# A state-space scan with the GpSimd product for four states at once, and the second step's inputs loaded first

## The chip, the cores and the metric

The kernel runs on one core of one Trainium2 chip. The metric is the device time of one execution in microseconds (us), of which the median over several runs is taken; lower is better. The engines are named as in the profile: PE is TensorE (matrix products), DVE is VectorE, ACT is ScalarE, POOL is GpSimd, SP is SyncE, which here issues every DMA.

## What is computed

Two layers of a network on images of 96 channels and 128 x 128 points, batch 2. The first layer mixes the points with a selective state-space scan (Mamba) along four orders of the points: rows, rows reversed, columns, columns reversed. Each order has 192 inner channels with 16 states each. Cut to the part that the change touches:

```python
def _mamba(x, in_w, conv_w, conv_b, xproj_w, dt_w, dt_b, A_log, Dp, outp_w):
    xz = x @ in_w.T
    xc, z = jnp.split(xz, 2, axis=-1)
    ...
    xc = jax.nn.silu((conv + conv_b[None, :, None]).transpose(0, 2, 1))
    xdbl = xc @ xproj_w.T
    ...
    dt = jax.nn.softplus(dt_raw @ dt_w.T + dt_b)
    A = -jnp.exp(A_log)
    def step(h, t):
        dt_t, u_t, B_t, C_t = t
        dA = jnp.exp(dt_t[:, :, None] * A)
        h = dA * h + dt_t[:, :, None] * B_t[:, None, :] * u_t[:, :, None]
        y = jnp.einsum('bds,bs->bd', h, C_t)
        return (h, y)
    ...
    y = ys.transpose(1, 0, 2) + Dp * xc
    y = y * jax.nn.silu(z)
    return y @ outp_w.T
```

A layer norm stands in front of it; the four results are projected, added and put on the input. A small two-layer network (FFN) with 8-bit products follows, then the second layer: a 3 x 3 convolution and a second FFN, each with a layer norm.

## The kernel before

For each of the two batches three stages run one after the other: `normalize` (layer norm, written to DRAM by rows as xnr and by columns as xnc), `mamba`, and `ffn_and_conv`. Nearly all of the time is in `mamba`.

**Steps and units.** `mamba` works in steps of 512 points (T). There are 64 steps in a batch: 32 blocks for the first pair of orders (rows and columns, forwards), then 32 for the second pair (backwards). The 2 x 192 channels of a pair of orders fill three groups (g = 0, 1, 2) of 128 partitions. A unit is two states of one group, so that a step has 24 units: group 0 is units 0 to 7, group 1 units 8 to 15, group 2 units 16 to 23. A quad is two units in a row, four states, starting at an even unit.

**What a unit does.** `decay` (L353): ScalarE makes two exponentials, dA, into a PSUM tile `da` of which there are three. `b_part`: GpSimd multiplies dt * u with a row of B in place (L345, 128 x 1024), and where the step is not the first of its pair it adds, with a small instruction (L347, 128 x 2), the decayed state of the step before to the first column. `scan` (L357): VectorE runs the recurrence along the 512 points, one instruction per state. `behind`: VectorE multiplies the states with the row of C (L431), ScalarE keeps the last column as the state for the next step (L432, `hst`), and TensorE sums the states of a group into y by products with the identity (L361, `sums`). For two units of each step, unit 2 and unit 10 (BY_POOL), the product with C is made by GpSimd (`by_pool`, L364), and their sums come three units later. At a group's end VectorE multiplies y with the gate (`gated`, L368), and TensorE and ScalarE project and collect it (L376, L378, L384).

**Rows.** B and C of a step lie in DRAM as rows (`bcd`); one DMA brings a quad of rows to all 128 partitions (L341, 1 MB). B has four such buffers and is fetched three quads ahead, C has three and is fetched two ahead. All DMAs stand in SP's one queue in the order of the program: in an even unit first the fetch of B, at its end the fetch of C.

**The prologue of a step** is the list `at` in `prologue`: the loads of its inputs (`load`, L220 or, for the first block, L218), three convolutions by products on TensorE (`conv`, L204), copied out by ScalarE (`conv_out`, L231), two silus (L251, L252 with the loads of their tables), B, C and dt from xc (L258, L264, L269, L276), the softplus in pieces on ScalarE (L281 to L292) and four small products of 512 columns per group on GpSimd (`dt_q`, `dt_log`, `dt_sum`, `dt_u`, L295 to L305), and the entering state (L310, L313). An entry (m, where, f) is put into unit m of the step before, so that a step's prologue runs under the scans of the step before it. Group 1 passes through a tile with its partitions in another order, `mix_xc` or `mix_sz`, and two DMAs put them in place (L248). Only the first step's prologue runs ahead of all scans, and the second step's, whose loads would belong to unit -2, is put in at unit 0.

**Order.** The order of instructions on each engine is written out by hand: it is the order in which the loop at the end of `mamba` calls them, unit after unit: the fetch of B, `feed` (b_part of the unit two ahead), the prologue's entries for place 0, the first scan, `behind` of the unit before, `feed_decay` (decay of the unit two ahead), the second scan, the fetch of C, and the entries for place 1. An instruction that waits holds up everything behind it on its engine.

Of the kernel before, what the change touches and what calls it, by code (L numbers as in the profile page):

```python
# [10 lines left out]
F32 = mybir.dt.float32  # L11
# [4 lines left out]
ALU = mybir.AluOpType  # L16
# [7 lines left out]
T = 512  # L24
# [10 lines left out]
AHEAD = 2  # L35
# [6 lines left out]
def tile_metaformer(ctx: ExitStack, tc: tile.TileContext, a: dict, out: bass.AP):  # L42
    nc = tc.nc
# [135 lines left out]
    def mamba(acc, xnr, xnc):  # L179

        with ExitStack() as st:
            pool = lambda n, bufs, **kw: st.enter_context(tc.tile_pool(name=n, bufs=bufs, **kw))
            io, one, two, gen = pool("io", 1), pool("one", 1), pool("two", 2), pool("gen", 4)
            ps_w, ps_y, ps_m = (pool(n, k, space=PSUM) for n, k in (("ps_w", 3), ("ps_y", 1), ("ps_m", 1)))
            rows_d = pool("rows_d", 3, space=DRAM)

# [1 line left out]
            enter = one.tile([128, NG, S], F32, name="enter")  # L188
# [18 lines left out]
            def prologue(pi, i, d):  # L207
# [19 lines left out]
                def conv_out(g):  # L227
                    if g == 1:
                        d["xc"] = two.tile([128, NG, T], F32, name="xc")
                    t = mixed("xc") if g == 1 else d["xc"][:, g, :]  # L230
                    nc.scalar.activation(t, d["ps"], AF.Identity, bias=convb[:, pi, g : g + 1])  # L231
# [4 lines left out]
                def gate_out(g):  # L236
                    if g == 1:
                        d["sz"] = two.tile([128, NG, T], F32, name="sz")
                    nc.scalar.copy(mixed("sz") if g == 1 else d["sz"][:, g, :], d["ps"])

                def mixed(name):
                    d["mix", name] = one.tile([128, T], F32, name=f"mix_{name}")
                    return d["mix", name]

                def mix(name):
# [89 lines left out]
            def row_tile(d, g, s, k, ahead):  # L335

                t = gen.tile([128, 4, T], F32, name=f"row{k}", bufs=ahead + 1)

                src = d["bcd"][k, s // 4] if g == 1 else d["bcd"][k, s // 4, g // 2 : g // 2 + 1]
                n = src.shape[0]  # L340
                nc.sync.dma_start(t, src[None].broadcast_to((128 // n, n, 4, T)))  # L341
                return t

            def b_part(i, d, g, s, b):
                nc.gpsimd.tensor_tensor(b, d["dtu"][g][:, None, :].broadcast_to((128, 2, T)), b, ALU.mult)  # L345
                if i > 0:
                    nc.gpsimd.tensor_tensor(b[:, :, 0], b[:, :, 0], enter[:, g, s : s + 2], ALU.add)  # L347

            def decay(pi, d, g, s):

# [5 lines left out]
            def scan(j, da, b, h):  # L356
                nc.vector.tensor_tensor_scan(h[:, j, :], da[:, j, :], b[:, j, :], 0.0, ALU.mult, ALU.add)  # L357
# [29 lines left out]
            steps = [(pi, i) for pi in range(2) for i in range(NT)]  # L387
            units = [(g, s) for g in range(NG) for s in range(0, S, 2)]
            nu = len(units)
            total = nu * len(steps)  # L390
            state = [{} for _ in steps]
            todo = {}

            def later(k, where, f, *args):
                todo.setdefault((k, where), []).append(partial(f, *args))

            def issue(k, where):
                for f in todo.pop((k, where), ()):
                    f()

            for k, where, f in prologue(*steps[0], state[0]):
                if k < nu:
                    f()
                else:
                    later(k - nu, where, f)
            bs, cs, das, hs = {}, {}, {}, {}

            def fetch(k, n, ahead, m):
                if k < total:
                    t = row_tile(state[k // nu], *units[k % nu], n, ahead)  # L410
                    m[k], m[k + 1] = t[:, 0:2, :], t[:, 2:4, :]

            def feed(k):
                if k < total:
                    n = k // nu
                    b_part(steps[n][1], state[n], *units[k % nu], bs[k])

            def feed_decay(k):
                if k < total:
                    n = k // nu  # L420
                    das[k] = decay(steps[n][0], state[n], *units[k % nu])
# [3 lines left out]
            def behind(k):  # L425

                n, u = divmod(k, nu)
                (pi, i), d, (g, s) = steps[n], state[n], units[u]
                h, c = hs.pop(k), cs.pop(k)
                if (g, s) not in BY_POOL:  # L430
                    nc.vector.tensor_tensor(c, h, c, ALU.mult)  # L431
                nc.scalar.copy(hst[:, g, s : s + 2], h[:, :, T - 1])  # L432
                if s == 0:
                    if k > 0:
                        pn, pu = divmod(k - 1, nu)
                        gated(steps[pn][0], state[pn], units[pu][0], ys.pop(k - 1))
                    y = ps_y.tile([128, T], F32, name="y")
                    nc.tensor.matmul(y, dmat[:, pi, g, :], d["xc"][:, g, :], start=True, stop=False)  # L438
                else:
                    y = ys.pop(k - 1)  # L440
                ys[k] = y
                if (g, s) in BY_POOL:
                    later(k + 1, 1, by_pool, h, c)
                    later(k + 3, 1, sums, s, y, c)
                else:
                    sums(s, y, c)
                if k == total - 1:
                    gated(pi, d, g, y)
                if s == S - 2 and g > 0:
                    later(k + 3, 0, project, pi, i, d, g)  # L450
                    later(k + 3, 1, collect, pi, d, g)

            for m, (n, ahead) in ((bs, (0, B_AHEAD)), (cs, (1, C_AHEAD))):
                for k in range(ahead):
                    fetch(2 * k, n, ahead, m)
            for k in range(AHEAD):
                feed(k)
                feed_decay(k)
            for k in range(total + 6):
                n, u = divmod(k, nu)  # L460

                ahead = 1 if k == 0 else n + 2 if u == nu - 2 else len(steps)
                if ahead < len(steps):
                    for m, where, f in prologue(*steps[ahead], state[ahead]):
                        later(max(k, (ahead - 1) * nu + m), where, f)
                if k % 2 == 0:
                    fetch(k + 2 * B_AHEAD, 0, B_AHEAD, bs)
                feed(k + AHEAD)
                issue(k, 0)
                if k < total:  # L470
                    (g, s) = units[u]
                    da, b = das.pop(k), bs.pop(k)
                    hs[k] = b if (g, s) in BY_POOL else da
                    scan(0, da, b, hs[k])
                if 0 < k <= total:
                    behind(k - 1)
                feed_decay(k + AHEAD)
                if k < total:
                    scan(1, da, b, hs[k])
                if k % 2 == 0:  # L480
                    fetch(k + 2 * C_AHEAD, 1, C_AHEAD, cs)
                issue(k, 1)
# [102 lines left out]
    for b in range(NB):  # L585
        xnr = dpool.tile([C, L], F32, name="xnr")
        xnc = dpool.tile([C, L], F32, name="xnc")
        normalize(b, acc, xnr, xnc)
        mamba(acc, xnr, xnc)
        ffn_and_conv(b, acc)  # L590
# [71 lines left out]
```

## Time and profile before

| What | Value |
|---|---|
| Median of 3 runs | 12191.46 us (12177.44 to 12192.11) |
| Profiled execution | 12201.18 us, its span 12199.4 us |
| VectorE busy over the span | 10961.9 us |
| GpSimd busy over the span | 10388.1 us |
| TensorE busy over the span | 10593.4 us |
| ScalarE busy over the span | 8592.7 us |
| First scan of batch 0 | 145.5 us into the span |
| First step of batch 0, first scan to the next step's | 96.1 us |
| Most frequent length of a step | 83.2 us |
| Mean granted TensorE clock | 0.975 |

A group's row in the profile reads: line, engine, operation, output<-inputs, shape, number; then the busy time of the group and the mean of one in ns; then the idle time of the engine just ahead of them and what ended most of it. A row of the timeline reads: start, duration, engine, line, operation, tiles, shape, number, and in brackets the idle time ahead of it with its releaser. A wait for several things is put down to the one that came last by the profile's records.

### The profile page before, as it was taken

To read this page: it belongs to the slowest core of one execution; us is meant where nothing else is said; L and a number is where in the kernel's file an instruction comes from. 1 tells how busy PE (TensorE), PEld (TensorE's weight loads), DVE (VectorE), ACT (ScalarE), POOL (GpSimd) and SP (SyncE) were. 2 spreads that over 40 slices of the span, in tenths; PEclk is the share of its full clock that TensorE was granted. 3 is DMA by queue.
4 is the path that set the end of the run, shared out by engine and by line. 5 is a ranking of instruction groups with operands and counts; after the bars stand their busy time and mean duration, and the time that the engine had idled before them with its cause. 6 is when DMAs were issued, how large, how long until landed. Compare 5 with 4: busy or idle time off the path is not lost. (4 is left out here: it accounts for less than half of the span.)

```text
span 12199.4 us, 100157 instructions
## 1 busy us (share of the span) xinstructions
PE 10593.4 (87%) x24208; PEld 4009.0 (33%) x24208; DVE 10961.9 (90%) x10624; ACT 8592.7 (70%) x15110; POOL 10388.1 (85%) x8360
## 2 busy tenths in 40 slices
PE   7888888888888888888978888888888888888889
PEld 2333333333333333333323333333333333333333
DVE  5999999999999999995469999999999999999954
ACT  6777777777777777765567777777777777777655
POOL 4999999999999999991159999999999999999911
PEclk8999999999999999999989999999999999999999
DMA  6887888888878878871068888878877878878700
GB/s 237 310 321 306 312 319 312 314 318 313 315 307 311 319 304 316 314 307 43 26 231 311 310 315 312 320 312 312 320 303 311 315 312 313 310 305 317 305 32 13
DMA packets 539204, 3417.36 MB, mean 280 GB/s; under 512 B 67276, under 2 KB 68396, under 8 KB 140696
## 3 DMA queue, kind: packets, MB, share of 16 engines
q1 hardware_dynamic: 538616, 3410.94, 72.5%
q8 instruction: 195, 3.19, 0.1%
q14 instruction: 393, 3.22, 0.1%
HBM read 3289.04 MB, written 54.53 MB: 274 GB/s over the span
## 5 line engine op out<-in xcount | busy, mean ns | idle before, releaser
L345 POOL TENSOR_TENSOR row<-dtu,row 128x1024 f32<-128x1024 f32 x3072 | 7235.6, 2356 | 262.2 <-DMA row<-bcd 212.3
L357 DVE TENSOR_TENSOR_SCAN da<-da,row 128x512 f32<-128x512 f32 x5632 | 6649.6, 1215 | 509.8 <-POOL row L347 166.1
L361 PE MATMUL y<-row,ident 128*128 128x512 f32 x12288 | 5956.1, 618 | 1135.8 <-DVE row L431 1131.4
L353 ACT ACTIVATE da<-dt,amat 128x512 f32<-128x512 f32 x6144 | 4249.9, 692 | 286.4 <-DVE row L357 99.3
L361 PEld LDWEIGHTS y<-row,ident 128*128 128x128 f32 x12288 | 2265.7, 193 | 4646.6 <-issue 2284.6
L431 DVE TENSOR_TENSOR row<-da,row 128x1024 f32<-128x1024 f32 x2816 | 3395.9, 1206 | 3.2 <-DMA row<-bcd 3.1
L432 ACT COPY hst<-da 128x2 f32<-128x2 f32 x2816 | 435.4, 155 | 1450.9 <-DVE row L431 1436.5
L204 PE MATMUL misc<-xa,inx 96*64 96x512 f32 (+1 forms) x2048 | 950.5, 607 | 133.1 <-DMA xa<-xnr 97.5
L556 POOL TENSOR_TENSOR acc<-acc,y 96x512 f32<-96x512 f32 x128 | 147.6, 1153 | 987.0 <-DVE y L555 972.6
L204 PE MATMUL misc<-xb,inx 96*64 96x512 f32 (+1 forms) x2048 | 949.7, 607 | 1.6 <-ACT xc L231 1.6
L347 POOL TENSOR_TENSOR row<-row,enter 128x2 f32<-128x2 f32 x2976 | 577.4, 194 | 233.4
L357 DVE TENSOR_TENSOR_SCAN row<-da,row 128x512 f32<-128x512 f32 x512 | 617.0, 1205 | 0.0
L364 POOL TENSOR_TENSOR row<-row,row 128x1024 f32<-128x1024 f32 x256 | 602.7, 2354 | 1.2 <-issue 0.6
L568 PE MATMUL pc<-pad,kw 96*96 96x512 f32 x1152 | 566.8, 593 | 0.0
L438 PE MATMUL y<-xc,dmat 128*128 128x512 f32 x768 | 432.1, 645 | 145.8 <-DVE sz L368 145.8
L295 POOL TENSOR_TENSOR q<-e,q 128x512 f32<-128x512 f32 x384 | 487.3, 1269 | 76.6 <-ACT q L292 71.5
L231 ACT ACTIVATE xc<-misc,convb 128x512 f32<-128x512 f32 x256 | 175.9, 687 | 525.8 <-PE misc L204 525.8
L204 PEld LDWEIGHTS misc<-xa,inx 96*64 96x64 f32 (+1 forms) x2048 | 326.8, 165 | 643.3 <-issue 470.1
L301 POOL TENSOR_TENSOR dt<-dt,ln 128x512 f32<-128x512 f32 x384 | 488.2, 1271 | 30.1
L298 POOL TENSOR_TENSOR ln<-ln,q 128x512 f32<-128x512 f32 x384 | 488.3, 1272 | 0.2
L305 POOL TENSOR_TENSOR dtu<-dt,xc 128x512 f32<-128x512 f32 x384 | 487.9, 1271 | 0.2
L378 PE MATMUL misc<-sz,gmat 128*96 128x512 f32 x1024 | 483.5, 594 | 0.0
(81 smaller groups left out, 9124.5 us busy)
## 6 DMA issues: line engine op xcount, KB each, us to landing
row<-bcd SPq DMA_DIRECT2D x3072, 1024.0 KB, 7.0
xc<-mix_xc SPq DMA_DIRECT2D x256, 128.0 KB, 5.3
sz<-mix_sz SPq DMA_DIRECT2D x256, 128.0 KB, 5.4
xa<-xnr SPq DMA_DIRECT2D x124, 193.1 KB, 5.3
xb<-xnc SPq DMA_DIRECT2D x124, 193.1 KB, 5.5
bcd<-rows SPq DMA_DIRECT2D x128, 128.0 KB, 6.5
acc<-in_x_dram SPq DMA_DIRECT2D x16, 768.0 KB, 8.6
xnr<-xn SPq DMA_DIRECT2D x16, 768.0 KB, 4.3
```

The lines of the kernel that those rows point to most:

```text
L204: nc.tensor.matmul(ps[rows, :], w(PAIRS[pi][d], k, lo, hi), src[d][:, k : k + T], **se)
L298: nc.gpsimd.tensor_tensor(d["ln"], d["ln"], d["q"], ALU.add)
L301: nc.gpsimd.tensor_tensor(d["dt"][g], d["dt"][g], d["ln"], ALU.add)
L305: nc.gpsimd.tensor_tensor(dtu, d["dt"][g], d["xc"][:, g, :], ALU.mult)
L345: nc.gpsimd.tensor_tensor(b, d["dtu"][g][:, None, :].broadcast_to((128, 2, T)), b, ALU.mult)
L347: nc.gpsimd.tensor_tensor(b[:, :, 0], b[:, :, 0], enter[:, g, s : s + 2], ALU.add)
L353: nc.scalar.activation(da[:, j, :], d["dt"][g], AF.Exp, scale=amat[:, pi, g, s + j : s + j + 1])
L357: nc.vector.tensor_tensor_scan(h[:, j, :], da[:, j, :], b[:, j, :], 0.0, ALU.mult, ALU.add)
L361: nc.tensor.matmul(y, ident, c[:, j, :], start=False, stop=s + j == S - 1)
L364: nc.gpsimd.tensor_tensor(c, h, c, ALU.mult)
L431: nc.vector.tensor_tensor(c, h, c, ALU.mult)
L568: nc.tensor.matmul(pc, kw[:, t, :], rows, start=t == 0, stop=t == 8)
```

## The change

GpSimd's `b_part` handles a quad: one product of 128 x 2048 and one add of 128 x 4, called only in even units, in front of that unit's prologue entries. The two mix tiles become one. The pool of the inputs xa and xb has two buffers, and the entries of a step's prologue that fall ahead of unit 0, which are the second step's loads, are issued at once, ahead of the first fetches of rows. Entries of later steps keep their units.

```diff
--- before.py
+++ after.py
@@ -180,7 +180,7 @@
 
         with ExitStack() as st:
             pool = lambda n, bufs, **kw: st.enter_context(tc.tile_pool(name=n, bufs=bufs, **kw))
-            io, one, two, gen = pool("io", 1), pool("one", 1), pool("two", 2), pool("gen", 4)
+            io, one, two, gen = pool("io", 2), pool("one", 1), pool("two", 2), pool("gen", 4)
             ps_w, ps_y, ps_m = (pool(n, k, space=PSUM) for n, k in (("ps_w", 3), ("ps_y", 1), ("ps_m", 1)))
             rows_d = pool("rows_d", 3, space=DRAM)
 
@@ -239,7 +239,7 @@
                     nc.scalar.copy(mixed("sz") if g == 1 else d["sz"][:, g, :], d["ps"])
 
                 def mixed(name):
-                    d["mix", name] = one.tile([128, T], F32, name=f"mix_{name}")
+                    d["mix", name] = one.tile([128, T], F32, name="mix")
                     return d["mix", name]
 
                 def mix(name):
@@ -342,9 +342,9 @@
                 return t
 
             def b_part(i, d, g, s, b):
-                nc.gpsimd.tensor_tensor(b, d["dtu"][g][:, None, :].broadcast_to((128, 2, T)), b, ALU.mult)
+                nc.gpsimd.tensor_tensor(b, d["dtu"][g][:, None, :].broadcast_to((128, 4, T)), b, ALU.mult)
                 if i > 0:
-                    nc.gpsimd.tensor_tensor(b[:, :, 0], b[:, :, 0], enter[:, g, s : s + 2], ALU.add)
+                    nc.gpsimd.tensor_tensor(b[:, :, 0], b[:, :, 0], enter[:, g, s : s + 4], ALU.add)
 
             def decay(pi, d, g, s):
 
@@ -403,17 +403,31 @@
                     f()
                 else:
                     later(k - nu, where, f)
-            bs, cs, das, hs = {}, {}, {}, {}
+
+            def prepare(n):
+                if n < len(steps):
+                    for m, where, f in prologue(*steps[n], state[n]):
+                        k = (n - 1) * nu + m
+                        if k < 0:
+                            f()
+                        else:
+                            later(k, where, f)
+
+            prepare(1)
+            bs, cs, das, hs, quads = {}, {}, {}, {}, {}
 
             def fetch(k, n, ahead, m):
                 if k < total:
                     t = row_tile(state[k // nu], *units[k % nu], n, ahead)
                     m[k], m[k + 1] = t[:, 0:2, :], t[:, 2:4, :]
+                    if n == 0:
+                        quads[k] = t
 
             def feed(k):
+
                 if k < total:
                     n = k // nu
-                    b_part(steps[n][1], state[n], *units[k % nu], bs[k])
+                    b_part(steps[n][1], state[n], *units[k % nu], quads.pop(k))
 
             def feed_decay(k):
                 if k < total:
@@ -453,19 +467,17 @@
             for m, (n, ahead) in ((bs, (0, B_AHEAD)), (cs, (1, C_AHEAD))):
                 for k in range(ahead):
                     fetch(2 * k, n, ahead, m)
+            feed(0)
             for k in range(AHEAD):
-                feed(k)
                 feed_decay(k)
             for k in range(total + 6):
                 n, u = divmod(k, nu)
-
-                ahead = 1 if k == 0 else n + 2 if u == nu - 2 else len(steps)
-                if ahead < len(steps):
-                    for m, where, f in prologue(*steps[ahead], state[ahead]):
-                        later(max(k, (ahead - 1) * nu + m), where, f)
+                if u == nu - 2:
+
+                    prepare(n + 2)
                 if k % 2 == 0:
                     fetch(k + 2 * B_AHEAD, 0, B_AHEAD, bs)
-                feed(k + AHEAD)
+                    feed(k + AHEAD)
                 issue(k, 0)
                 if k < total:
                     (g, s) = units[u]
```

## The prediction

> **What bounds the kernel now.** I read the busy shares first, then the costliest groups, then a table of stretches, then the timeline of one step engine by engine, because the shares alone name two engines at once.
>
> ```profile
> PE 10593.4 (87%) x24208; PEld 4009.0 (33%) x24208; DVE 10961.9 (90%) x10624; ACT 8592.7 (70%) x15110; POOL 10388.1 (85%) x8360
> ...
> L345 POOL TENSOR_TENSOR row<-dtu,row 128x1024 f32<-128x1024 f32 x3072 | 7235.6, 2356 | 262.2 <-DMA row<-bcd 212.3
> L357 DVE TENSOR_TENSOR_SCAN da<-da,row 128x512 f32<-128x512 f32 x5632 | 6649.6, 1215 | 509.8 <-POOL row L347 166.1
> ...
> L347 POOL TENSOR_TENSOR row<-row,enter 128x2 f32<-128x2 f32 x2976 | 577.4, 194 | 233.4
> ```
>
> ```profile
> 1000.00:2000.00 1000.00, 874.15 (x1985) 331.02 (x1986) 964.31 (x871) 727.89 (x1289) 955.23 (x776) 0.99 0.80 313
> ```
>
> In a scanning stretch (columns: PE, its loads, VectorE, ScalarE, GpSimd) VectorE is busy 96%, GpSimd 96%, TensorE 87%. The largest named wait of the scans is for GpSimd's small add (166.1 us). This looks like a kernel that a faster GpSimd would help by up to 510 us. The timeline of one step says otherwise. I take the step whose first scan is at 2003.94; the next one's is 83.2 later, and 66 of the 122 undisturbed steps take 83.2 within 0.1. Times "into the step" count from that scan. The step's three VectorE stalls:
>
> ```profile
> 2017.96 1.23 DVE L357 TENSOR_TENSOR_SCAN da<-da,row 128x512 f32<-128x512 f32 x1 [0.86 <-POOL row L347]
> ...
> 2025.56 1.23 DVE L357 TENSOR_TENSOR_SCAN da<-da,row 128x512 f32<-128x512 f32 x1 [0.76 <-POOL row L347]
> ...
> 2036.45 1.23 DVE L357 TENSOR_TENSOR_SCAN da<-da,row 128x512 f32<-128x512 f32 x1 [0.68 <-ACT hst L432]
> ```
>
> The first two (units 4 and 6) are GpSimd's. The third, unit 9, is there in every step at 0.4 to 0.7 us, also where the first is missing. What ends it is on TensorE and ScalarE:
>
> ```profile
> 2019.65 3.60 PE L204 MATMUL misc<-xa,inx 96*128 96x512 f32 x8
> 2023.09 1.88 PE L361 MATMUL y<-row,ident 128*128 128x512 f32 x4
> 2024.80 3.60 PE L204 MATMUL misc<-xb,inx 96*128 96x512 f32 x8
> ```
>
> ```profile
> 2028.44 0.69 ACT L231 ACTIVATE xc<-misc,convb 128x512 f32<-128x512 f32 x1 [1.43 <-PE misc L204]
> 2029.03 0.15 ACT L432 COPY hst<-da 128x2 f32<-128x2 f32 x1
> 2029.21 1.42 ACT L353 ACTIVATE da<-dt,amat 128x512 f32<-128x512 f32 x2
> 2030.65 1.28 ACT L251 ACT_TABLE_LOAD   x1
> ...
> 2034.93 1.42 ACT L353 ACTIVATE da<-dt,amat 128x512 f32<-128x512 f32 x2
> ```
>
> TensorE has no idle time from 2.4 to 41 us into the step: the last sums of the old step, three convolutions, a projection and the sums of units 0 to 6. Its third convolution ends at 24.4, ScalarE copies it out, makes one decay, does the silu (4.1 us with its two table loads) and only then the decay of unit 9, ready at 32.4; the scan starts at 32.5. So from product 23 of the old step (1.1) to scan 9 (32.5) runs a chain of 31.4 us in which GpSimd has no part. Unit 6 is held by it as well: its decay is ready at 21.5, the scan started at 21.6. From scan 9 to the next product 23 VectorE runs without a gap, 51.8 us. Chain and run are 83.2: the period.
>
> GpSimd meets this period with room to spare:
>
> ```profile
> 2039.26 2.35 POOL L345 TENSOR_TENSOR row<-dtu,row 128x1024 f32<-128x1024 f32 x1 [0.74 <-DMA row<-bcd]
> ```
>
> Before unit 12 it waits for rows (35.4 into the step, mean 1.7 over the steps). Their load stands in SP's queue behind a load that waits for TensorE's sums of units 2 and 3 (28.3), again the chain.
>
> **The Trainium skill.** Its page "GPSIMD Engine Reference", section 3.1 Elementwise, gives 4497 ns for a tensor_tensor add of 2048 fp32 elements. The trace has no such size, but 1271 ns at 512, 2356 at 1024 and 194 at 2: 2.12 ns an element and 187 fixed, so 4.52 us; they agree. Its page "Perfetto Trace Analysis", section GPSIMD Engine Instruction, advises start-to-start spacing for GpSimd, which I use: product and add come every 2.58 us. Its page "DMA: Bandwidth & Descriptors", section Anatomy of one DMA, says a semaphore wait is held by the issuing sequencer before dispatch; the trace agrees, with SP's 5297.7 us of waiting on TensorE in one queue.
>
> **The change part by part.** 1. *Quads.* Two products and two adds (2 x 2.58 = 5.16 us) become 4.52 + 0.08 gap + about 0.15 = 4.75; saved 0.41 to 0.45 a quad, 12 quads, about 5 us of GpSimd's 82 per step. The price is granularity: the even unit waits for 4.75 instead of 2.58. With GpSimd's order and spacings (small products 1.22 to 1.3, by_pool 2.3) the quad's readiness against its first scan in the 83.2 us step, starting from the rows at 35.5:
>
> unit 12: 40.3 against 42.2; 14 (behind by_pool): 47.3 / 49.0; 16: 52.2 / 55.7; 18 (behind three small products): 60.8 / 63.0; 20: 66.8 / 69.7; 22: 75.4 / 76.5; next step's 0: 81.6 / 83.2; 2: 87.5 / 90.5; 4: 96.1 / 96.1; 6: 103.2 / 102.9; 8: 108.1 / 109.9; 10: 112.9 / 118.6; then rows at 118.7 again.
>
> Only unit 6 is 0.3 late, where ScalarE's decay is later still (104.7). So the 2.4 us of GpSimd stall at units 4 to 6 go, and the same time comes back as waits for ScalarE at 5, 6 and 9. Gain in an 83.2 us step: nothing. If the chain cover were gone it would be up to 2.4 us a step.
>
> 2. *Steps where GpSimd is late elsewhere.* Going through the scans, 12 steps lose 0.5 to 1.4 us at units 21 to 23 to the small add, 11.8 us in all. There VectorE is exposed. Putting their own row times into the list above, the worst quad is 0.0 to 0.1 late at unit 22 and 0.3 at 14: some 10 to 12 us gained; bounds 0 and 14.
>
> 3. *Late inputs.* Some 35 steps are longer because TensorE waits for xa (0.1 to 3.9 us each). The second buffer does not help: in the instruction order of both kernels the load of every later step stands at the same place of SP's queue, and in before it waits there for no reader of the old buffer; it is issued 2 us ahead of the step and lands 5 to 10 us later. Gain 0; bounds -10 and +10.
>
> 4. *The second step's inputs.* In before they are issued behind seven row loads of 1 MB:
>
> ```profile
> 138.03 3.70 SPq L341 DMA_DIRECT2D row<-bcd  x7
> 141.83 0.42 SPq L220 DMA_DIRECT2D xa<-xnr  x1
> ```
>
> ```profile
> 159.14 1.09 PE L204 MATMUL misc<-xa,inx 96*64 96x512 f32 x1 [14.74 <-DMA xa<-xnr]
> ```
>
> ```profile
> 168.32 1.23 DVE L357 TENSOR_TENSOR_SCAN da<-da,row 128x512 f32<-128x512 f32 x1 [9.70 <-ACT da L353]
> ```
>
> TensorE stands 14.7 us, ScalarE behind it (10.8 in front of L231), VectorE behind that. The first step takes 96.1 us in batch 0, 95.3 in batch 1; without stalls VectorE needs 79.7 (first unit has no gate). Stalls there: 1.4, 9.7, 1.2, 2.3, 1.0, and 0.1 restarting after each. In after, the two loads (0.45 us each to issue, 0.39 MB, 1 us at the 2.48 us per MB of the landings) go ahead of the rows: rows 1 us later, first quad 2.2 later than the first pair: first scan 3.1 us later. The convolution can start when ScalarE frees the misc bank, about 147.5 instead of 159.1. Left over are ScalarE waits: in the first step it has two extra dt groups (4 us each) and two silus by unit 12, about 34 us in VectorE's 30 up to unit 9, of which two units of lead cover most: 2 to 3 us. Gain 16.4 - 3.1 - 2.5 = 10.8 us, twice: 21.6; bounds 14 and 26.
>
> 5. *One mix buffer for both.* The 512-column tile is written at units 2 and 13 and its two copies land within some 5 us: 35 us of slack, cost 0. Waits of the state copies on DMAs disappear; they cost nothing now.
>
> Sum: 0 + 11.8 + 0 + 21.6 = 33.4 us. Profiled execution 12201.18 - 33.4 = 12168; that execution is 9.7 above the median of the runs, so 12191.46 - 33 = 12158.
>
> **Rivals.** A: *GpSimd was the bound.* For it: the named waits of 166 us and 96% busy. Then the 2.4 us a step go, 126 x 2.4 = 300: about 11870. Against: unit 9's wait in every step, TensorE without a gap. Chance 0.08. B (slower): *the quad gates VectorE at units 12 to 22*, where nothing covers. The smallest lead is 1.1 at unit 22, six quads after the rows; it is used up when a quad costs 0.18 more, 4.9 with its add. At 5.1 it would be 1.0 to 1.2 us a step, +140 - 22: about 12310. For it: a size never traced, and DMA jitter: rows land up to 2 us late in a tenth of the steps, 7 in the worst. Against: a straight line through three sizes. Chance 0.12. C: *the start gives nothing net* because ScalarE's load and the later first quad eat it: 12180 or so. Chance 0.12.
>
> **Numbers.** The forecast has 0.68. A difference of 0.2% (24 us) is about what a measurement can tell from no change; the forecast is 33 +- 12, beyond it nine times in ten. Faster 0.61 + 0.08 = 0.69, same 0.07 + 0.11 = 0.18, slower 0.13. The forecast alone spans 12130 to 12185; with C and the lesser degrees of A and B, 12100 to 12198.
>
> **What would show it.** Right: L345 x1536 at about 4.5 us; steps still 83.2 apart; fewer waits of L357 for the add, more for ScalarE; unit 9's stall near 2 to 3 us; first steps near 85 us; xa waits fewer by two, of 14 us. Wrong: periods under 82 (A); waits for the add at units 12 to 22 (B); first steps over 92 (C).

## The result, and the profile after

| | before | after |
|---|---|---|
| Median | 12194.74 us (20 runs, 12177.44 to 12248.8) | 12164.91 us (20 runs, 12131.31 to 12198.56) |
| Ratio to before | | 0.9971, 95% interval 0.9961 to 0.9981 |

By the medians the change gains 29.8 us; 33 were forecast. The ratio in the table is not the quotient of the two medians (0.9976); by it the gain is 35 us, with an interval from 23 to 48. The two profiled executions hide this: their spans are 12199.4 and 12196.8 us, because the profiled execution of after, 12198.56 us, is the slowest of its 20. So the traces are compared stretch by stretch and step by step, not by their spans.

First the page of after: busy time by engine, then the groups that answer to those shown of before.

```profile
PE 10601.0 (87%) x24208; PEld 4012.8 (33%) x24208; DVE 10962.5 (90%) x10624; ACT 8585.5 (70%) x15110; POOL 9908.7 (81%) x5336
...
L345 POOL TENSOR_TENSOR row<-dtu,row 128x2048 f32<-128x2048 f32 x1536 | 6949.9, 4525 | 820.8 <-DMA row<-bcd 658.5
L357 DVE TENSOR_TENSOR_SCAN da<-da,row 128x512 f32<-128x512 f32 x5632 | 6650.2, 1215 | 509.8 <-ACT da L353 187.3
```

A quad costs 4525 ns, as the straight line through three sizes said. GpSimd has 479.4 us less work (10388.1 to 9908.7) and stands idle for most of it: its products now wait 658.5 us for rows instead of 212.3. The idle time of these scans is 509.8 us, as before. That it agrees to the tenth is chance: the first two steps of the batches lost 28 us of it and the last ones 2, while the waits ahead of the two first scans grew by 10 and the steps between by 20, through inputs that came late (below). What the change did in the usual step is to put other names behind the idle time, which the view of VectorE's waits shows best (who waited, for whom, us in total, times, the longest). After:

```profile
DVE da L357 <- ACT da L353: 187.3, 190, 3.6
DVE da L357 <- ACT hst L446: 157.8, 124, 1.6
DVE da L357 <- POOL row L345: 103.3, 6, 51.8
...
DVE da L357 <- POOL row L347: 49.8, 100, 1.0
```

The wait for the small add fell from 166.1 to 49.8 us, and the two waits for ScalarE rose from 88.9 and 72.8 to 187.3 and 157.8. The timeline of VectorE in one step of after, whose first scan is at 2000.60, has its stalls at the same three units as before (4, 6 and 9):

```profile
2014.01 1.23 DVE L357 TENSOR_TENSOR_SCAN da<-da,row 128x512 f32<-128x512 f32 x1 [0.25 <-POOL row L347]
...
2022.23 1.23 DVE L357 TENSOR_TENSOR_SCAN da<-da,row 128x512 f32<-128x512 f32 x1 [1.38 <-ACT hst L446]
...
2033.03 1.23 DVE L357 TENSOR_TENSOR_SCAN da<-da,row 128x512 f32<-128x512 f32 x1 [0.59 <-ACT da L353]
```

Into the step these are 13.4, 21.6 and 32.4 us; in before they were 14.0, 21.6 and 32.5. Unit 4 starts 0.6 us sooner and loses it at unit 6, which starts at the same moment in both kernels. The usual step is 83.13 us against 83.20. In all of the 122 steps between the batches' starts and ends, unit 6 now waits for ScalarE (1.28 us in the mean) and so does unit 9 (0.59 us); GpSimd's add is still what ends the stall at unit 4 in 91 of them. GpSimd's own order came out as worked out: in this step the quads of units 12, 16, 18 and 22 are ready at 40.2, 52.2, 60.9 and 75.5 us, where the prediction's list has 40.3, 52.2, 60.8 and 75.4.

Most of what was gained is at the start of each batch. VectorE's timeline of after, first scan, and then the two stalls of the first step that are left up to unit 9 (a third, of 0.45 us, comes at unit 22):

```profile
151.40 3.61 DVE L357 TENSOR_TENSOR_SCAN da<-da,row 128x512 f32<-128x512 f32 x3 [51.78 <-POOL row L345]
...
176.89 1.23 DVE L357 TENSOR_TENSOR_SCAN da<-da,row 128x512 f32<-128x512 f32 x1 [0.43 <-POOL row L345]
...
180.81 1.23 DVE L357 TENSOR_TENSOR_SCAN da<-da,row 128x512 f32<-128x512 f32 x1 [0.44 <-ACT da L353]
```

The 9.70 us stall is gone. By the distances of the steps' first scans, the first steps take 80.8 us in both batches (96.1 and 95.3 before) and the second ones 83.1 (84.5 and 84.4).

### The profile page after: what moved, and what is told of

Its sections match the earlier page's. It is cut to its first block, busy times and chain, and to the rows that moved or that the text cites. A ratio compares the mean times of both kernels' runs of the same rounds, so it can differ in the third digit from the quotient of the medians.

```text
span 12196.8 us, 95712 instructions
## 1 busy us (share of the span) xinstructions
PE 10601.0 (87%) x24208; PEld 4012.8 (33%) x24208; DVE 10962.5 (90%) x10624; ACT 8585.5 (70%) x15110; POOL 9908.7 (81%) x5336
## 5 line engine op out<-in xcount | busy, mean ns | idle before, releaser
L345 POOL TENSOR_TENSOR row<-dtu,row 128x2048 f32<-128x2048 f32 x1536 | 6949.9, 4525 | 820.8 <-DMA row<-bcd 658.5
L357 DVE TENSOR_TENSOR_SCAN da<-da,row 128x512 f32<-128x512 f32 x5632 | 6650.2, 1215 | 509.8 <-ACT da L353 187.3
L124 DVE TENSOR_TENSOR xq<-xm,rs 96x512 fp8e5<-96x512 f32 x128 | 87.9, 687 | 388.0 <-ACT rs L120 387.9
```

## The experiments

The two theories: TensorE's and ScalarE's chain sets the step, so that only the start gains; or GpSimd's work sets it, so that the quads gain. Ratios are to before, each measured beside it on the same chip. "Usual step" is the most frequent length, read from the first scans of the 122 steps that are neither at a batch's start nor at its end. The median of before moved between 12189.86 and 12201.45 us from one session to the next, so a difference between the medians of two experiments is good to some 10 us only.

**The early loads alone.** Second input buffer, one mix tile, early loads; b in pairs.

```diff
 # after.py
-                nc.gpsimd.tensor_tensor(b, d["dtu"][g][:, None, :].broadcast_to((128, 4, T)), b, ALU.mult)
+                nc.gpsimd.tensor_tensor(b, d["dtu"][g][:, None, :].broadcast_to((128, 2, T)), b, ALU.mult)
...
-                    nc.gpsimd.tensor_tensor(b[:, :, 0], b[:, :, 0], enter[:, g, s : s + 4], ALU.add)
+                    nc.gpsimd.tensor_tensor(b[:, :, 0], b[:, :, 0], enter[:, g, s : s + 2], ALU.add)
...
                     fetch(k + 2 * B_AHEAD, 0, B_AHEAD, bs)
-                    feed(k + AHEAD)
+                feed(k + AHEAD)
```

> The early loads, the second input buffer and the one mix tile, with b still made in pairs. Theory (TensorE and ScalarE set the step, the start is what is gained): the first scan 3 to 4 us later, the first step near 82 us instead of 96, twice; 20 to 28 us faster than before, ratio about 0.998; waits of the scans for the small add stay near 166 us. Rival (GpSimd's work sets the step, the quads are what is gained): 5 us or less, ratio 0.9995 to 1.

Measured: 12185.14 us, ratio 0.9991 (0.9984 to 0.9999); 16 us gained by the medians, beside 12201.45, and 11 by the ratio. First scan at 150.2, first steps 82.7 and 82.6 us, usual step 83.20, the wait for the small add 152.1 us. The direction and the place are those of the theory; the size is under the 20 to 28 us expected, in part because the first scan comes 4.7 us late instead of 3 to 4. It is more than the rival allows, but the interval reaches to it.

**The quads alone.** The loads and buffers of before, b in quads as in the change's diff.

```diff
 # before.py
-                nc.gpsimd.tensor_tensor(b, d["dtu"][g][:, None, :].broadcast_to((128, 2, T)), b, ALU.mult)
+                nc.gpsimd.tensor_tensor(b, d["dtu"][g][:, None, :].broadcast_to((128, 4, T)), b, ALU.mult)
...
-                feed(k + AHEAD)
+                    feed(k + AHEAD)
```

> The quads alone, with the loads and buffers of before. Theory: the usual step stays at 83.1 to 83.2 us, GpSimd's waits are exchanged for ScalarE's; 2 us lost at each start, 6 to 12 us gained in the steps where GpSimd was late at units 21 to 23: 0 to 12 us faster, ratio 0.999 to 1.000; first steps still about 95 us. Rival (GpSimd sets the step): 25 us or more faster, ratio 0.998 or less.

Measured: 12177.55 us, ratio 0.9981 (0.9971 to 0.9991), 24 us gained, where 0 to 12 were expected. That is a miss upwards, and by the total alone the rival, which named 25 us or more, is nearer. The steps tell what the trace can account for. The usual step is 83.13 us: 0.07 for 122 steps are 8.5 us, which no step of the prediction had. First scan at 147.7, 2.2 late as worked out; the first steps 93.4 and 93.2 us, 2 to 3 less than in before, the second ones 83.2 and 83.1. Together that is about 12 to 14 us, inside the interval (11 to 35 us) at its low end; where the rest comes from, if it is there, is open. The product of this ratio and the one above is 0.9972, so within the noise the two halves add up to the whole. Neither theory's claim to all of the gain stands; but the quads' share doesn't come out of the stalls at units 4 and 6. The wait for the small add fell to 57.0 us, and the waits for ScalarE took its place:

```profile
DVE da L357 <- ACT hst L434: 158.0, 124, 1.7
DVE da L357 <- ACT da L353: 156.1, 172, 9.1
DVE da L357 <- POOL row L345: 96.8, 4, 48.8
DVE da L357 <- POOL row L347: 57.0, 114, 1.3
```

**Less work for GpSimd, no quads.** The small add is left out of before, so the entering state is not in the scans.

```diff
 # before.py
-                if i > 0:
-                    nc.gpsimd.tensor_tensor(b[:, :, 0], b[:, :, 0], enter[:, g, s : s + 2], ALU.add)
```

> Before with GpSimd's small add (L347) left out, so that the state of the step before does not enter the scans; 0.23 us less of GpSimd per unit, 5.4 us per step, without the quads' coarser grain. Theory: the usual step stays at 83.2 us, only the late steps gain, 10 to 20 us in all, ratio 0.9984 to 0.9992. Rival (GpSimd sets the step): the 2.4 us of stall a step go, 250 to 300 us, ratio 0.976 to 0.98.

Measured: 12191.43 us, ratio 0.9988 (0.9980 to 0.9995), as expected. The usual step is 83.20 us, to the hundredth that of before, though GpSimd has the 577 us of the small adds less to do. Its groups and VectorE's waits:

```profile
L345 POOL TENSOR_TENSOR row<-dtu,row 128x1024 f32<-128x1024 f32 x3072 | 7187.3, 2356 | 1035.3 <-DMA row<-bcd 819.3 <-DVE sz L366 199.7 <-ACT hst L430 9.7
L355 DVE TENSOR_TENSOR_SCAN da<-da,row 128x512 f32<-128x512 f32 x5632 | 6642.6, 1214 | 508.4 <-POOL row L345 202.1 <-ACT da L351 150.8 <-ACT hst L430 84.0
```

GpSimd's work turned into waiting for rows (212.3 to 819.3 us), and the scans' idle time did not move (509.8 to 508.4). A wait put down to GpSimd's product is still the largest name; it is no cause, as the step did not get shorter. Unit 9 waits 0.67 us in all of the 122 steps (0.6 us in 121 of them in before). This is what rules out GpSimd as the bound of before.

**The inputs sooner.** After, with each later step's inputs loaded at unit -8 instead of -2; the second buffer allows it.

```diff
 # after.py
-                at = [(-2, 1, load), (2, 1, partial(mix, "xc")), (6, 1, partial(silu, "xc"))]
+                at = [(-8, 1, load), (2, 1, partial(mix, "xc")), (6, 1, partial(silu, "xc"))]
...
-                if u == nu - 2:
+                if u == nu - 8:
```

> After with each later step's inputs loaded at unit -8 instead of -2, which the second buffer allows. Theory (steps over 83.2 us come from xa landing late, up to 6.7 us a step): TensorE's waits for xa vanish but for the two at the batches' starts, at least 115 of 122 steps are under 83.5 us, 80 to 130 us faster than after, 110 to 160 faster than before, ratio 0.987 to 0.991. Rival (the lateness is of all DMAs and comes up elsewhere, in rows): under 40 us faster than after, ratio over 0.994, with waits of GpSimd or VectorE for rows in its place.

Measured: 12078.82 us (12073.04 to 12081.04), ratio 0.9897 (0.9881 to 0.9913): 86 us under after by the medians, 90 by the ratios. The view of TensorE's waits has two for the inputs left, at the two batches' starts. In after it had 33, two of them at the starts:

```profile
PE misc L204 <- DMA xa<-xnr: 108.0, 33, 28.4
```

With the inputs sooner:

```profile
PE misc L204 <- DMA xa<-xnr: 28.4, 1, 28.4
PE misc L204 <- DMA xb<-xnc: 28.3, 1, 28.3
```

107 of the 122 steps are within 0.3 us of the usual 83.13 (71 in after), a few under the 115 expected. The time lost ahead of unit 9, over that of the usual step, fell from 122 to 2 us; what is left over is 9 us behind it, nearly all at unit 22 and GpSimd's. The lateness did not come up elsewhere. The spread of the runs fell from 67 us (20 runs) to 8 (5 runs): late inputs are most of what makes executions of after differ. The mean granted clock goes along with this: it went from 0.973 to 0.978 over the runs of after, lower in the longer ones, and was 0.977 or 0.978 in all five here. The edit doesn't touch it, but which of the two drives the other isn't shown.

**A shorter chain, in pairs and in quads.** Inputs at unit -10; the first convolution is made at unit -2, where TensorE has idle time, the second at 1, the third at 4 instead of 5; the move of the first through the mix tile comes sooner with it. Once with pairs (early-only kernel), once with quads (after).

```diff
-                at = [(-2, 1, load), (2, 1, partial(mix, "xc")), (6, 1, partial(silu, "xc"))]
+                at = [(-10, 1, load), (-1, 1, partial(mix, "xc")), (6, 1, partial(silu, "xc"))]
...
-                for g, k in ((1, 1), (0, 3), (2, 5)):
+                for g, k in ((1, -2), (0, 1), (2, 4)):
...
-                if u == nu - 2:
+                if u == nu - 10:
```

> b in pairs, as in the early-only kernel, with the inputs loaded at unit -10 and the first and third convolutions taken out of TensorE's crowded stretch (first at unit -2 instead of 1, second at 1 instead of 3, third at 4 instead of 5). Theory: the chain that set the step is about 2.5 us shorter, so the step falls until GpSimd, 82.3 us of work with pairs, sets it: usual step 82.3 to 83.0 us, waits of the scans for the small add grow over 166 us; 12010 to 12080 us, ratio 0.984 to 0.990. Rival (the chain isn't what sets the step, or VectorE alone is): 83.2 or 80.5 us a step with pairs and quads alike.

> The same moves with the quads of after. Theory: GpSimd needs only 77 us, so the step falls to VectorE's 80.3 us and what is left of ScalarE's waits: usual step 80.4 to 81.6 us, 1 to 2.4 us a step under the pairs' kernel, 11760 to 11900 us, ratio 0.964 to 0.976; the quads, worth some 20 us before, are worth 120 to 290 here. Rival (quads are worth nothing with this order either): within 30 us of the pairs' kernel.

Measured: pairs 11962.37 us, ratio 0.9815 (0.9801 to 0.9828); quads 11860.28 us, ratio 0.9730 (0.9717 to 0.9744). The steps are 82.1 us in the mean with pairs and 81.3 with quads, the usual steps 82.15 and 81.0. The pairs' kernel is some 50 us faster than expected, and the quads' advantage is 102 us, under the 120 of the range: GpSimd's need with pairs, set at 82.3 us a step, is 82.1 or less. The kernel with the inputs sooner alone kept the usual step of 83.13 us and is 218 us slower than the quads' kernel here, so the shorter step is the convolutions' doing and not the inputs'. The stretch from 1000 to 2000 us (PE, its loads, VectorE, ScalarE, GpSimd), pairs first:

```profile
1000.00:2000.00 1000.00, 884.28 (x2019) 334.11 (x2018) 983.72 (x889) 745.39 (x1312) 974.20 (x793) 0.99 0.83 320
```

```profile
1000.00:2000.00 1000.00, 897.03 (x2034) 338.90 (x2033) 992.90 (x899) 754.17 (x1330) 937.31 (x503) 0.98 0.84 323
```

With pairs GpSimd is busy 97.4%, and what is left is not waiting: its products wait for rows 33.0 us in the whole run, 28 of them at the starts. VectorE's and GpSimd's waits with pairs:

```profile
DVE da L357 <- POOL row L347: 111.7, 242, 1.3
...
POOL row L345 <- DMA row<-bcd: 33.0, 10, 14.1
```

The scans wait for the add at units 4 and 6 alone. In total these waits are under before's 166 us, where over 166 were expected: here GpSimd does set the step, and the waits named after it are fewer than in before, where it didn't. With quads VectorE is busy 99.3% and the wait for the add is 32.5 us. With the chain out of the way, the same quads are worth 102 us. The quads' kernel is the fastest of all, 2.5% under after.

**A quad that costs more.** After, with a spare GpSimd product behind each quad's add.

```diff
 # after.py
+            spare = one.tile([128, 128], F32, name="spare")
+            nc.gpsimd.memset(spare, 0.0)
...
                     nc.gpsimd.tensor_tensor(b[:, :, 0], b[:, :, 0], enter[:, g, s : s + 4], ALU.add)
+                nc.gpsimd.tensor_tensor(spare, spare, spare, ALU.mult)
```

> After with one more GpSimd product of 128 x 128 on a spare tile behind each quad's add, about 0.46 us a quad (estimated from the rows at 2, 512 and 1024 columns), 5.5 us a step: GpSimd then has as much work as in before, in quads. Theory of the exposed places: at unit 22 five of these, 2.3 us, stand against a lead of 1.1, and nothing covers there: usual step 84.2 to 84.8 us with waits for the add at unit 22, 130 to 200 us slower than after, 12290 to 12370 us, ratio 1.008 to 1.014. Rival (a quad has slack to spare as GpSimd's total of 83 us is under the step): usual step 83.1 to 83.3 us, under 30 us slower than after, ratio 0.997 to 1.000.

Measured: 12314.36 us, ratio 1.0108 (1.0091 to 1.0125): 149 us over after's median. The spare product took 399 ns, where the line through other sizes had given 0.46 us. Groups and waits of that kernel:

```profile
L350 POOL TENSOR_TENSOR spare<-spare 128x128 f32<-128x128 f32 x1536 | 612.2, 399 | 0.0
```

```profile
DVE da L360 <- POOL row L349: 391.6, 320, 2.0
DVE da L360 <- POOL row L347: 111.4, 10, 51.4
```

In 120 of the 122 steps unit 22 waits for the add, 0.90 us each, 108 us in all. Most of the rest of the 391.6 us, 231 at unit 4 and 40 at unit 6, lies in the stretch from unit 4 to unit 9, where ScalarE holds the scans too. The 75 steps in which TensorE doesn't wait for inputs are 84.35 us in the median, as expected: some 1.0 us over after's behind unit 9 and 0.3 ahead of it. All 122 steps are 85.0 us in the mean. So 0.4 us a quad turn the change into a loss, most of it at unit 22, where the list of the prediction had its smallest lead without cover, although GpSimd's whole work is only 1.3% over that of before (9908.7 + 612.2 us against 10388.1).

## Why the prediction was right

- *The bound.* Right. The step is set by TensorE's convolutions, ScalarE's silu and the decays behind them. Shown from both sides: less work for GpSimd left the step at 83.20 us; a shorter chain brought it to 81.0. The experiments moved only the convolutions; ScalarE's part of the chain is read from the timelines.
- *Quads.* Cost right (4.52 foretold, 4525 ns), and so is the argument that nothing is gained at units 4 to 6. One detail was wrong: unit 9's stall was to grow to 2 or 3 us; it stayed 0.59. Unit 6, which the text had as held by ScalarE too, takes all of the time back.
- *0.07 us a step*, 8.5 us in all, was not foreseen. The kernels with quads and the old order have it, and none of those with pairs. At unit 9 the scan starts 0.03 us after its decay instead of 0.10. In before the scan of an odd unit also waits for GpSimd, in after for ScalarE alone; that this is the cause is argued, not shown.
- *Steps with GpSimd late.* Mis-sized: 10 to 12 us expected; the loss at units 9 to 23 went from 12.7 to 9.0 us. The lead at unit 22 was put at -0.1 to 0.0 in such steps, and it is -0.4 to -0.7 in nearly all of after's.
- *Late inputs.* Right that the second buffer doesn't help: TensorE waits for xa 33 times in after, 35 in before. The time lost ahead of unit 9 is 122 us in after's profiled execution and 90 in before's, a difference as large as the change. But after's execution lies 33.7 us over its median and before's 6.4; without that some 88 and 84 us would be left (an estimate), which are alike.
- *The start.* The sum is right by luck, as its terms are not: first scan 5.9 us later (3.1 expected), stalls left in the first step about 1 us (2.5 expected), and the second step 1.3 us shorter, which was not in the working. In batch 0: 5.9 - 15.3 - 1.3 = -10.7 us, against the -10.8 of the sum. The first rows take 7.1 us from issue to landing behind the two input loads, instead of about 5. The sign "first steps near 85 us" does not fit the prediction's own terms either, which make 79.7 + 2.5 = 82.2; it was 80.8.
- *Sum.* Start 22, usual step 8.5, late steps 3.7: 34 us, where the medians show 29.8 and the ratio 35. The working had 21.6, 0 and 11.8. That the total came out so near is in part luck, as the last two miss in opposite directions. The experiments split it otherwise than the working too: 16 us for the early loads alone, with 20 to 28 expected, and 24 for the quads alone, with 0 to 12 expected.

## What to carry to other kernels

A wait's name says what came last there, not what sets the pace: look for the stall that is in every period, also where the named one is missing, and follow that one back. Taking work from an engine that isn't on this chain turns into idle time on it; the same saving was worth 24 us with the chain in place and 102 us with it shortened and the inputs sooner. When a buffer is added, ask what it now allows to be moved: issuing the inputs six units sooner was worth 86 us more, over twice the whole change.

## What was not expected of the hardware

The input loads of a step, 0.39 MB, were issued at the same point of each step and landed between 5 and 10 us later. In about a quarter of the steps (32 of 122 in before, 31 in after) this was late enough for TensorE to wait, up to 3.9 us, and the step with that wait was 7.6 us longer than usual. Issued six units sooner, the same loads took longer to land, 9.1 us in the median instead of 5.2 (xa), but no step waited for them. The runs' spread came down from 67 us to 8 with it, so most of the difference between executions of after was in these landings.
